# Column halves of the array for nearly all matmuls of a window-attention and Fourier kernel

## The chip, the cores and the metric

The kernel runs on one core of a Trainium2 chip. The metric is device time in microseconds (us), from the first to the last instruction of one execution; lower is better. The core has a matrix engine (TensorE, "PE" in the profile, with its weight loads as "PEld"), a vector engine (VectorE, "DVE"), a scalar engine (ScalarE, "ACT"), GpSimd ("POOL"), and SyncE ("SP"), which issues the DMA transfers. TensorE computes `lhsT.T @ rhs`: a weight load puts `lhsT` into the array of 128 rows by 128 columns, then the columns of `rhs` stream through it, and the result goes to PSUM, which here is used as 8 banks of 512 f32 values per partition. [...]

## The reference

Input `x` has shape (32, 56, 56, 128) in f32: 32 images of 56 by 56 tokens with 128 channels. Two layers, each with a residual, everything in f32:

```python
# layer 0: group norm, shifted 7x7 window attention with 4 heads of 32 channels
qkv = (win @ w_qkv.T)...                       # win: windows of 49 tokens of roll(gn(x), (-3, -3))
attn = softmax(q * scale @ k.T + bias + mask)  # per window and head, 49 x 49
out = (attn @ v) @ w_proj.T + b_proj           # rolled back
x = x + out
# layer 1: group norm, a Fourier mix along width and along height, a feed-forward
xy = idct_w(einsum(dct_w(gn(x))[first 32 modes], w0))
xx = idct_h(einsum(dct_h(gn(x))[first 32 modes], w1))
x = x + relu((xx + xy) @ W1 + b1) @ W2 + b2    # 128 -> 512 -> 128
```

## The kernel before

An image is 8 rows of 8 windows. The kernel walks over 32 x 8 rows ("cycles"); in one cycle the parts of several stages, for different rows and images, stand side by side so that TensorE always has work. Each engine runs its instructions in the written order. The matmuls of one cycle come in groups by the part of the array that they use, and the functions have names after that: full (128 rows x 128 columns), half columns (128x64), quarters (64x64), eighths (64x32).

```python
CONV_BEGIN = NWR + 2        # NWR = 8: the cycle in which layer 1 of image 0 begins
def attn_bank(): return bank("pa", 4)      # PSUM: 4 banks for attention,
def conv_bank(): return bank("pc", 4)      # 4 for layer 1, each in turn

def attn_qk(im, i, first):                 # row i of image im
    pq = attn_bank()
    nc.tensor.matmul(pq[:, :n], lhsT=im.w[:, 0:C], rhs=src, ...)            # L363, n = 392 or 393
    nc.scalar.activation(q[:, :RT], pq[:, :RT], AF.Identity, ...)
    pk = attn_bank()
    nc.tensor.matmul(pk[:, :n], lhsT=im.w[:, C:2*C], rhs=src, ...)          # L370
    ...                                     # k copied by ScalarE, then by VectorE
def attn_v(im, i, r):                       # L395: 8 windows, on column halves
def attn_scores(im, i, r):                  # L417: 64x64; then VectorE adds bias and mask (L425)
def attn_max(r):                            # VectorE maximum (L435), GpSimd subtracts it (L436)
def attn_exp(r):                            # ScalarE (L442)
def attn_divide(r):                         # VectorE sum (L447), reciprocal, GpSimd product (L450)
def attn_transpose(im, i, r):
    for hf in range(2):
        pt = attn_bank()
        for h in range(NH):
            nc.tensor.transpose(pt[...], a[...], ident[:PW, :PW])           # L461, full
        aT = work.tile([P, 4, P], F32, tag="aT", name="aT")
        ...                                 # copied out by VectorE, then ScalarE
def attn_values(im, i, r):                  # L486: attention x v, 64 matmuls of 64x32
def attn_project(im, i):                    # L528: output projection, 128*112
def transform(...)                          # L637: cosine transform, column halves
def mix(...)                                # L671: mode mix, column halves
def modes_back(...)                         # L710: inverse transform, 64x64
def ff_in(im, g):                           # group g: 512 (five times), 320, 256 tokens
    for f in range(NF):
        ph = conv_bank()
        nc.tensor.matmul(ph[:, :n], lhsT=wff1[:, f*P:(f+1)*P], rhs=xff[:, t0:t0+n], ...)  # L753
        ...                                 # relu on ScalarE (L761)
def ff_out(im, g):
    for c, m in enumerate(chunks):          # m = 128 tokens, in the group of 320 a last one of 64
        for f in range(NF):
            nc.tensor.matmul(pf[:m, ...], lhsT=im.hid[f][:, c*P:c*P+m], rhs=wff2[:, f],
                             start=(f == 0), stop=(f == NF - 1))            # L773
...
# one cycle, from cycle CONV_BEGIN on
full_first(cycle, norm)      # attn_qk(cycle), statistics, ff_in, attn_divide(cycle - 1)
if not row(cycle - 2)[0]: ...
elif any(c in FF_AT for _, c in fourier(cycle)):        # 7 of 8 cycles
    quarters(cycle)          # attn_scores(cycle), modes_back
    attn_max(cycle)
    half_columns(cycle)      # attn_v(cycle), transform or mix
    eighths(cycle)           # attn_values(cycle - 2)
else:
    half_columns(cycle); quarters(cycle); eighths(cycle); attn_max(cycle)
full_last(cycle, norm)       # attn_transpose(cycle - 1), ff_out, attn_project(cycle - 2),
                             # transposes of the next image (L262), attn_exp(cycle)
```

Of the kernel before, what the change touches and what calls it, by code (L numbers as in the profile page):

```python
# [41 lines left out]
FF_GROUPS = (HB, HB, HB, HB, HB, 320, 256)  # L42
FF_AT = (7, 8, 9, 10, 12, 13, 14)
PW = JP + WT
CONV_BEGIN = NWR + 2


@with_exitstack
def swin_fourier_kernel(
# [23 lines left out]
    const = ctx.enter_context(tc.tile_pool(name="const", bufs=1))  # L73
    big = ctx.enter_context(tc.tile_pool(name="big", bufs=1))
    work = ctx.enter_context(tc.tile_pool(name="work", bufs=2))
    small = ctx.enter_context(tc.tile_pool(name="small", bufs=4))
    psum = ctx.enter_context(tc.tile_pool(name="psum", bufs=2, space=bass.MemoryType.PSUM))
    dram = ctx.enter_context(tc.tile_pool(name="dram", bufs=2, space=bass.MemoryType.DRAM))

# [11 lines left out]
    def chunks_of(t, b, n0, n1):  # L91

        tok = t[b].rearrange("h w c -> (h w) c")
        wrap = (S - SS) // 2
        if n0 < wrap:
            e = min(n1, wrap)
            part = tok[SS * S + n0 * TC : SS * S + e * TC].rearrange("(n p) c -> p n c", p=TC)
            yield n0, e, slice(0, TC), part
        if n0 <= wrap < n1:
            yield wrap, wrap + 1, slice(0, S), t[b, S - 1].unsqueeze(1)  # L100
            yield wrap, wrap + 1, slice(S, TC), t[b, 0].unsqueeze(1)
        if n1 > wrap + 1:
            a = max(n0, wrap + 1)
            t0 = (2 * a + SS) % S * S
            part = tok[t0 : t0 + (n1 - a) * TC].rearrange("(n p) c -> p n c", p=TC)
            yield a, n1, slice(0, TC), part


    def load_image(b):
# [53 lines left out]
            )  # L163
    nc.sync.dma_start(rpb[JP : JP + WT], rpb[0:WT])

    mask_sb = const.tile([P, 2, 2, WT], F32, tag="mask", name="mask")
    nc.vector.memset(mask_sb, 0.0)
    for hh in range(2):
        rows = slice(hh * JP, hh * JP + WT)
# [132 lines left out]
    def image_norm(im):  # L302
# [46 lines left out]
        nc.scalar.mul(im.w, wqkv, rstd)  # L349
        yield  # L350
        pb = attn_bank()
        nc.tensor.matmul(pb[:, 0:1], lhsT=wqkv[:, 2 * C :], rhs=nb, start=True, stop=True)
        im.bias = small.tile([P, 5], F32, tag="bqkv", name="bqkv")
        nc.vector.tensor_copy(im.bias[:, 2:3], pb[:, 0:1])
        yield
# [2 lines left out]
    def attn_qk(im, i, first):  # L358

        n = RT if i else RT + 1  # L360
        q, src = q_sb, im.xw[i][:, :n]
        pq = attn_bank()
        nc.tensor.matmul(pq[:, :n], lhsT=im.w[:, 0:C], rhs=src, start=True, stop=True)  # L363
        if i == 0:
            nc.scalar.mul(im.bias[:, 0:1], pq[:, RT:n], QS)
        nc.scalar.activation(  # L366
            q[:, :RT], pq[:, :RT], AF.Identity, bias=im.bias[:, 0:1], scale=QS
        )
        pk = attn_bank()
        nc.tensor.matmul(pk[:, :n], lhsT=im.w[:, C : 2 * C], rhs=src, start=True, stop=True)  # L370
        if i == 0:
            for u in range(2):
                nc.scalar.mul(im.bias[:, 3 + u : 4 + u], pk[:, RT:n], heads[:, u : u + 1])
        pk3 = pk[:, :RT].rearrange("p (w j) -> p w j", j=WT)
        nc.scalar.activation(  # L375
            k_sb[:, 0], pk3, AF.Identity, bias=im.bias[:, 3:4], scale=heads[:, 0:1]
        )
        if first:
            nc.scalar.activation(
                k_sb[:, 1], pk3, AF.Identity, bias=im.bias[:, 4:5], scale=heads[:, 1:2]  # L380
            )
        else:
# [71 lines left out]
    def attn_transpose(im, i, r):  # L454

        a = a_sb[r % 3]
        im.aT[i] = []
# [3 lines that stand above are left out]
                nc.tensor.transpose(  # L461
                    pt[:PW, h * P : h * P + PW],
                    a[:PW, h, 2 * hf : 2 * hf + 2].rearrange("p w j -> p (w j)")[:, :PW],
                    ident[:PW, :PW],
                )
            aT = work.tile([P, 4, P], F32, tag="aT", name="aT")
            src = pt[:PW].rearrange("p (m x) -> p m x", x=P)[:, :, :PW]
            if hf:
                nc.scalar.copy(aT[:PW, :, :PW], src)
            else:  # L470
                nc.vector.tensor_copy(aT[:PW, :, :PW], src)
            im.aT[i].append(aT)
# [48 lines left out]
    def attn_project(im, i):  # L521
# [3 lines left out]
        base = i // 2 * WS  # L525
        pp = attn_bank()
        for n in range(n0, n1):
            nc.tensor.matmul(  # L528
                pp[:TC, (n - n0) * C : (n - n0 + 1) * C],
                lhsT=oT[:, (n - base) * TC : (n - base + 1) * TC],  # L530
                rhs=wproj,
                start=True,
                stop=True,
            )
        piece = im.x[:, n0:n1]
        nc.vector.tensor_tensor(
# [9 lines left out]
    def attn_sums(im, i):  # L546
# [7 lines left out]
            op=ALU.add,  # L554
        )
        yield
        sq = work.tile([TC, 4, C], F32, tag="sq", name="sq", bufs=1)[:, : n1 - n0]
        nc.scalar.activation(sq, piece, AF.Square)
        nc.vector.tensor_reduce(
            im.part[:, 1, :, i],  # L560
# [7 lines left out]
    def fourier_stats(im):  # L568
# [7 lines left out]
        yield  # L576
        pg = attn_bank()

        nc.tensor.matmul(
            pg[:, : C // 2],  # L580
            lhsT=gmean,
            rhs=tot.rearrange("p k g -> p (k g)"),
            start=True,
            stop=True,
        )
        own = small.tile([P, 2, C // 4], F32, tag="own", name="own", bufs=1)
        nc.vector.scalar_tensor_tensor(
            out=own,
# [141 lines left out]
    def ff_in(im, g):  # L730
# [19 lines left out]
        im.hid = []  # L750
        for f in range(NF):
            ph = conv_bank()
            nc.tensor.matmul(  # L753
                ph[:, :n],
                lhsT=wff1[:, f * P : (f + 1) * P],
                rhs=xff[:, t0 : t0 + n],
                start=True,
                stop=True,
            )
            hf = work.tile([P, HB], F32, tag="hid", name="hid", bufs=NF)  # L760
            nc.scalar.activation(hf[:, :n], ph[:, :n], AF.Relu, bias=b1sb[:, f : f + 1])  # L761
            im.hid.append(hf)

    def ff_out(im, g):
# [5 lines left out]
        pf = conv_bank()  # L770
        for c, m in enumerate(chunks):
            for f in range(NF):
                nc.tensor.matmul(  # L773
                    pf[:m, c * C : (c + 1) * C],
                    lhsT=im.hid[f][:, c * P : c * P + m],
                    rhs=wff2[:, f],
                    start=(f == 0),
                    stop=(f == NF - 1),
                )
# [33 lines left out]

    images = {}

    def row(r):
# [10 lines left out]
            return [(c >= 6, c % 2 * 2 + j) for j in range(2)]  # L829
        return []  # L830

    def full_first(cycle, norm):
        last, j = row(cycle - 3)
        if last:
            sums = attn_sums(last, j)
            next(sums)
# [22 lines left out]
        if row(cycle - 1)[0]:  # L859
            attn_divide(cycle - 1)  # L860

    def half_columns(cycle):
        im, i = row(cycle)
        if im:
            attn_v(im, i, cycle)
        for im, c in fourier(cycle):
            if c == 0:
                for g in range(4):
# [19 lines left out]
                modes_back(im, width, g)  # L888

    def eighths(cycle):  # L890
        im, i = row(cycle - 2)
        if im:
            attn_values(im, i, cycle - 2)

    def transpose_next(cycle):


        im, i = row(cycle - 1)
        if im:
            attn_transpose(im, i, cycle - 1)  # L900

    def last_out(cycle):
        for im, c in fourier(cycle):
            if c in FF_AT:
                ff_out(im, FF_AT.index(c))

    def full_last(cycle, norm):
        transpose_next(cycle)
        next(norm)
        im, j = row(cycle - 2)  # L910
        if im:
            last_out(cycle)
            attn_project(im, j)
        next_image(cycle)
        if row(cycle)[0]:
            attn_exp(cycle)
        next(norm)

    def next_image(cycle):
        b, i = divmod(cycle, NWR)  # L920
        if b + 1 < NB:
            if i == 2:
                images[b + 1] = image_begin(b + 1)
            for j in {3: (0,), 4: (2,), 5: (4,), 6: (6,)}.get(i, ()):
                image_groups(images[b + 1], j)

    def first_rows(cycle, norm):
# [2 lines left out]
            attn_qk(im, i, True)  # L932
        if cycle:
            attn_exp(cycle - 1)
        last, j = row(cycle - 3)
        if last:
            attn_project(last, j)
        im2, i2 = row(cycle - 2)
        if im2:
            attn_transpose(im2, i2, cycle - 2)  # L940
# [2 lines left out]
        if im:  # L943
            attn_scores(im, i, cycle)
            attn_max(cycle)
        if im2:
            attn_values(im2, i2, cycle - 2)
        next(norm)
        if last:
            for _ in attn_sums(last, j):  # L950
                pass
# [2 lines left out]
        if cycle < NWR // 2:  # L954
            image_bias(im, 2 * cycle)
        next(norm)
        next_image(cycle)
        if cycle == CONV_BEGIN - 1:
            attn_exp(cycle)
            attn_project(im2, i2)  # L960
            transpose_next(cycle)
        next(norm)

    def nothing():
# [4 lines left out]
    with tc.manual_schedule(engines={ET.PE, ET.Activation, ET.DVE, ET.Pool}):  # L969
# [6 lines left out]
        for cycle in range(NB * NWR + CONV_BEGIN + FF_AT[-1] - NWR + 1):  # L976
            if cycle < CONV_BEGIN:
                first_rows(cycle, norm)
            else:
                full_first(cycle, norm)  # L980
                if not row(cycle - 2)[0]:
                    half_columns(cycle)
                    last_out(cycle)
                    quarters(cycle)
                elif any(c in FF_AT for _, c in fourier(cycle)):
                    quarters(cycle)
                    if row(cycle)[0]:
                        attn_max(cycle)
                    half_columns(cycle)
                    eighths(cycle)  # L990
                else:
                    half_columns(cycle)
                    quarters(cycle)
                    eighths(cycle)
                    if row(cycle)[0]:
                        attn_max(cycle)
                full_last(cycle, norm)
            b, i = divmod(cycle, NWR)
            norm = nothing()
            if i == NWR - 2 and b + 1 < NB:  # L1000
# [64 lines left out]
```

## Time and profile before

| | |
|---|---|
| time, median of 3 | 3666.67 us (3664.5 to 3670.33) |
| span of the profiled execution | 3661.5 us |
| TensorE clock granted | 0.997 of full |
| TensorE matmul records | 61184 |
| bytes moved by DMA | 388.93 MB, 106 GB/s |
| costliest groups: feed-forward output (L773) | 760.4 us busy, 6400 records |
| hidden layer (L753) | 710.7 us busy, 1792 records |
| transposes of the attention (L461) | 267.3 us busy, 2048 records |

An engine's busy time is the union of its instructions' intervals. Matmuls overlap in the array and the ends of their intervals are modelled, so what a matmul costs is read from the distance between the starts of neighbouring matmuls rather than from its length. In the lists of groups the shape behind the tile names is the part of the array used (rows*columns), and then the operand that streams (partitions x columns). L773 is line 773 of the kernel.

### The profile page before, as it was taken

Reading aid. Unit: us, or ns where it says so; the run is one execution under the profiler, and the core shown is the slowest. Engines: PE = TensorE matmul, PEld = TensorE weight load, DVE = VectorE, ACT = ScalarE, POOL = GpSimd, SP = SyncE. Lnnn points to the kernel's source line nnn. Section 1 sums busy time; section 2 is a strip of 40 time slices with the busy share of each in tenths; the row PEclk is TensorE's granted clock in tenths of the full one; section 3 lists DMA queues with packets and bytes.
Section 4 is the critical chain, followed back from the end, with each engine's and each line's share of the span. In section 5 each row is a group of like instructions: output and inputs, shape, how many; then the busy total and the mean of one; then the engine's idle time right before and its main releaser. Section 6 shows DMA issues by size and latency. Waiting matters only on the chain.

```text
span 3661.5 us, 139922 instructions
## 1 busy us (share of the span) xinstructions
PE 3603.5 (98%) x61184; PEld 2940.9 (80%) x61184; DVE 2224.1 (61%) x4739; ACT 2123.3 (58%) x4043; POOL 1372.0 (37%) x1421
## 2 busy tenths in 40 slices
PE   7899999999999999999999999999999999999999
PEld 5787888888888888888787888888887888888887
DVE  7766666566666566665666665666666666556641
ACT  5555555555655555565556555556555555655553
POOL 5433334333334333333333333334333333333321
PEclk9999999999999999999999999999999999999999
DMA  4334433443434444334434343443344343433333
GB/s 116 97 102 114 106 107 94 112 113 102 117 96 110 108 108 112 104 97 113 108 101 113 95 118 104 106 115 94 111 107 110 105 112 92 118 106 104 97 109 96
DMA packets 687268, 388.93 MB, mean 106 GB/s; under 512 B 39968, under 2 KB 657601, under 8 KB 686401
## 3 DMA queue, kind: packets, MB, share of 16 engines
q1 hardware_dynamic: 686045, 379.65, 38.3%
q8 instruction: 482, 7.90, 0.9%
q14 instruction: 130, 1.06, 0.1%
q10 hardware_dynamic: 611, 0.32, 0.0%
HBM read 218.29 MB, written 161.48 MB: 104 GB/s over the span
## 4 chain that ended last, share of the span: by engine, by line
PE 94%; ACT 2%; DVE 2%; DMA 1%; issue 1%; POOL 0%; SPq 0%; ACTq 0%; POOLq 0%; DVEq 0%
PE pc L773 19%; PE pc L753 17%; PE pa L395 7%; PE pa L461 7%; PE pc L671 6%; PE pc L637 6%; PE pa L528 6%; PE pa L417 6%; PE pa L486 5%; PE pa L363 5%; PE pc L710 5%; PE pa L370 4%; PE pa L262 2%; ACT k L375 1%; DVE k L383 1%
## 5 line engine op out<-in xcount | busy, mean ns | idle before, releaser
L773 PE MATMUL pc<-wff,hid 128*128 128x128 f32 x6400 | 760.4, 276 | 0.9 <-ACT hid L761 0.8
L773 PEld LDWEIGHTS pc<-wff,hid 128*128 128x128 f32 x6400 | 732.3, 190 | 9.4 <-issue 2.4
L450 POOL TENSOR_TENSOR a<-a,rs 128x784 f32<-128x784 f32 x256 | 389.5, 1522 | 874.0 <-DVE rs L449 869.5
L753 PE MATMUL pc<-xf,wff 128*128 128x512 f32 (+2 forms) x1792 | 710.7, 539 | 0.9 <-DVE xf L721 0.7
L753 PEld LDWEIGHTS pc<-xf,wff 128*128 128x128 f32 x1792 | 339.2, 190 | 310.1 <-issue 228.6
L761 ACT ACTIVATE hid<-pc,b1sb 128x512 f32<-128x512 f32 (+2 forms) x896 | 535.2, 644 | 83.0 <-PE pc L753 73.7
L436 POOL TENSOR_TENSOR a<-a,mx 128x784 f32<-128x784 f32 x256 | 389.2, 1520 | 437.0 <-DVE mx L435 430.6
L785 DVE TENSOR_TENSOR res<-pc,res 128x512 f32<-128x512 f32 (+3 forms) x257 | 144.0, 571 | 660.9 <-issue 476.9
L293 POOL TENSOR_TENSOR xl<-xl,bproj 112x512 f32<-112x512 f32 (+1 forms) x256 | 285.6, 1137 | 508.6 <-PE pa L262 508.6
L425 DVE TENSOR_TENSOR a<-pa,bm 128x392 f32<-128x392 f32 x512 | 259.5, 549 | 178.8 <-PE pa L417 178.7
L517 DVE TENSOR_SCALAR oT<-pa,bqkv 128x98 f32<-128x98 f32 (+2 forms) x768 | 170.4, 276 | 218.4 <-PE pa L486 218.4
L402 ACT COPY v<-pa 128x512 f32<-128x512 f32 x256 | 153.3, 599 | 256.9 <-PE pa L395 256.9
L743 POOL TENSOR_TENSOR res<-res,b2sb 128x512 f32<-128x512 f32 (+2 forms) x256 | 263.8, 1035 | 94.3 <-DMA res<-scr 94.3
L280 ACT COPY xw<-pa 128x392 f32<-128x392 f32 x128 | 62.3, 486 | 396.1 <-PE pa L262 396.1
L383 DVE TENSOR_SCALAR k<-pa,heads,bqkv 128x392 f32<-128x392 f32 x246 | 168.4, 685 | 202.4 <-ACT k L375 200.1
L417 PEld LDWEIGHTS pa<-k,q 64*64 64x64 f32 x8192 | 183.4, 132 | 133.6 <-DVE rs L449 45.5
L395 PE MATMUL pa<-wn,xw 128*64 128x128 f32 x4096 | 282.7, 281 | 3.9 <-DVE a L425 3.9
L366 ACT ACTIVATE q<-pa,bqkv 128x392 f32<-128x392 f32 x256 | 150.5, 588 | 218.8 <-PE pa L363 217.3
L461 PE MATMUL pa<-ident,a 113*113 113x113 f32 x2048 | 267.3, 273 | 5.3 <-POOL a L450 4.4
L442 ACT ACTIVATE a<-a 128x784 f32<-128x784 f32 x256 | 225.0, 879 | 74.2 <-POOL a L436 74.1
L395 PEld LDWEIGHTS pa<-wn,xw 128*64 128x64 f32 x4096 | 220.4, 137 | 53.8 <-ACT xw L275 16.2
L435 DVE TENSOR_REDUCE mx<-a 128x16 f32<-128x784 f32 x256 | 247.0, 965 | 5.5
(91 smaller groups left out, 6050.6 us busy)
## 6 DMA issues: line engine op xcount, KB each, us to landing
zscr<-z SPq DMA_DIRECT2D x512, 112.0 KB
htok<-scr SPq DMA_DIRECT2D x256, 196.0 KB
zT<-zscr SPq DMA_DIRECT2D x192, 256.0 KB
res<-scr SPq DMA_DIRECT2D x160, 256.0 KB
out_dram<-res SPq DMA_DIRECT2D x160, 256.0 KB
scr<-xl SPq DMA_DIRECT2D x128, 224.0 KB
xl<-in_x_dram SPq DMA_DIRECT2D x32, 784.0 KB
xl<-in_x_dram SPq DMA_DIRECT2D x32, 672.0 KB
```

Of the source, the lines that this page charges most:

```text
L293: nc.gpsimd.tensor_tensor(piece, piece, bproj.unsqueeze(1).to_broadcast([TC, e - a, C]), ALU.add)
L395: nc.tensor.matmul(pv[hs, j * C : (j + 1) * C], lhsT=im.xw[i][:, w * WT : w * WT + JP], rhs=im.w[:, 2 * C : 3 * C], start=True, stop=True,)
L417: nc.tensor.matmul(ps[hp][HALVES[e], pr * 2 * WT : (pr + 1) * 2 * WT], lhsT=q[cs, w * WT : w * WT + JP], rhs=k_sb[cs, :, w], start=True, s ...
L425: nc.vector.tensor_tensor(a[:, 2 * hp : 2 * hp + 2, :, 0:WT].rearrange("p u w j -> p w u j"), ps[hp][:, :RT].rearrange("p (w u j) -> p w u ...
L435: nc.vector.tensor_reduce(mx, a3, axis=AX.X, op=ALU.max)
L436: nc.gpsimd.tensor_tensor(a3, a3, mx.unsqueeze(2).to_broadcast([P, 2 * NWR, WT]), ALU.subtract)
L450: nc.gpsimd.tensor_tensor(a3, a3, rs.unsqueeze(2).to_broadcast([P, 2 * NWR, WT]), ALU.mult)
L461: nc.tensor.transpose(pt[:PW, h * P : h * P + PW], a[:PW, h, 2 * hf : 2 * hf + 2].rearrange("p w j -> p (w j)")[:, :PW], ident[:PW, :PW],)
L743: nc.gpsimd.tensor_tensor(res[:m, c0:c1], res[:m, c0:c1], b2sb[:m].unsqueeze(1).to_broadcast([m, c1 - c0, C]), ALU.add,)
L753: nc.tensor.matmul(ph[:, :n], lhsT=wff1[:, f * P : (f + 1) * P], rhs=xff[:, t0 : t0 + n], start=True, stop=True,)
L761: nc.scalar.activation(hf[:, :n], ph[:, :n], AF.Relu, bias=b1sb[:, f : f + 1])
L773: nc.tensor.matmul(pf[:m, c * C : (c + 1) * C], lhsT=im.hid[f][:, c * P : c * P + m], rhs=wff2[:, f], start=(f == 0), stop=(f == NF - 1),)
```

## The change

The change puts every matmul of the full array, except the transposes, on two column halves: a helper issues it as two matmuls of up to 64 weight columns each, with the same streamed operand, into the two halves of the partitions. The cycle then needs the full array only for transposes, and these are gathered: in every second cycle the transposes of two rows are done together, and those of the next image are done in two cycles instead of four. For that the attention product and the output projection run three rows behind the scores instead of two, layer 1 begins one cycle later, and `aT` has four buffers. Its purpose is that the array changes its shape less often. To make room in SBUF, the small tiles have two buffers instead of four, and the mask shares a work tile. The core of the diff (left out: the same replacement at the small statistics matmuls, the mask's tile, and the first rows):

```diff
-CONV_BEGIN = NWR + 2
+CONV_BEGIN = NWR + 3
-    small = ctx.enter_context(tc.tile_pool(name="small", bufs=4))
+    small = ctx.enter_context(tc.tile_pool(name="small", bufs=2))
+    def halved(dst, lhsT, rhs, start=True, stop=True):
+        for p in range(0, dst.shape[0], P // 2):
+            ps = slice(p, min(p + P // 2, dst.shape[0]))
+            nc.tensor.matmul(dst[ps], lhsT=lhsT[:, ps], rhs=rhs, start=start, stop=stop)
...
-        nc.tensor.matmul(pq[:, :n], lhsT=im.w[:, 0:C], rhs=src, start=True, stop=True)
+        halved(pq[:, :n], im.w[:, 0:C], src)
...
-        nc.tensor.matmul(pk[:, :n], lhsT=im.w[:, C : 2 * C], rhs=src, start=True, stop=True)
+        halved(pk[:, :n], im.w[:, C : 2 * C], src)
...
-            aT = work.tile([P, 4, P], F32, tag="aT", name="aT")
+            aT = work.tile([P, 4, P], F32, tag="aT", name="aT", bufs=4)
...
-            nc.tensor.matmul(
+            halved(
                 pp[:TC, (n - n0) * C : (n - n0 + 1) * C],
-                lhsT=oT[:, (n - base) * TC : (n - base + 1) * TC],
-                rhs=wproj,
...
-            nc.tensor.matmul(
-                ph[:, :n],
-                lhsT=wff1[:, f * P : (f + 1) * P],
-                rhs=xff[:, t0 : t0 + n],
+            halved(ph[:, :n], wff1[:, f * P : (f + 1) * P], xff[:, t0 : t0 + n])
...
-                nc.tensor.matmul(
+                halved(
                     pf[:m, c * C : (c + 1) * C],
-                    lhsT=im.hid[f][:, c * P : c * P + m],
-                    rhs=wff2[:, f],
+                    im.hid[f][:, c * P : c * P + m],
+                    wff2[:, f],
...
     def eighths(cycle):
-        im, i = row(cycle - 2)
+        im, i = row(cycle - 3)
...
+    def full(cycle):
+        for k in (2, 1) if cycle % 2 == 0 else ():
+            im, i = row(cycle - k)
+            if im:
+                attn_transpose(im, i, cycle - k)
+            if k == 2 and row(cycle)[0]:
+                attn_max(cycle)
+        next_groups(cycle)
+
+    def next_groups(cycle):
+        b, i = divmod(cycle, NWR)
+        if b + 1 < NB:
+            for j in {5: (0, 2), 6: (4, 6)}.get(i, ()):
+                image_groups(images[b + 1], j)
...
-    def full_last(cycle, norm):
-        transpose_next(cycle)
+    def halves_last(cycle, norm):
+        im, i = row(cycle)
+        if im:
+            attn_v(im, i, cycle)
+        if has_ff(cycle):
+            half_columns(cycle)
+        next_begin(cycle)
         next(norm)
-        im, j = row(cycle - 2)
+        im, j = row(cycle - 3)
         if im:
             last_out(cycle)
             attn_project(im, j)
-        next_image(cycle)
         if row(cycle)[0]:
             attn_exp(cycle)
...
-                full_first(cycle, norm)
-                if not row(cycle - 2)[0]:
+                halves_first(cycle, norm)
+                if not row(cycle - 3)[0]:
                     half_columns(cycle)
                     last_out(cycle)
                     quarters(cycle)
-                elif any(c in FF_AT for _, c in fourier(cycle)):
-                    quarters(cycle)
-                    if row(cycle)[0]:
-                        attn_max(cycle)
+                    continue
+                if not has_ff(cycle):
                     half_columns(cycle)
-                    eighths(cycle)
-                else:
-                    half_columns(cycle)
-                    quarters(cycle)
-                    eighths(cycle)
-                    if row(cycle)[0]:
-                        attn_max(cycle)
-                full_last(cycle, norm)
+                eighths(cycle)
+                quarters(cycle)
+                if row(cycle)[0] and cycle % 2:
+                    attn_max(cycle)
+                full(cycle)
+                halves_last(cycle, norm)
```

More of the change, by code (lines that the diff above doesn't have):

```diff
@@ L164, in swin_fourier_kernel @@
     nc.sync.dma_start(rpb[JP : JP + WT], rpb[0:WT])
-    mask_sb = const.tile([P, 2, 2, WT], F32, tag="mask", name="mask")
+    mask_sb = work.tile([P, 4, C], F32, tag="sq", name="mask", bufs=1).rearrange("p n c -> p (n c)")
+    mask_sb = mask_sb[:, : 4 * WT].rearrange("p (r k j) -> p r k j", r=2, k=2)
     nc.vector.memset(mask_sb, 0.0)
@@ L351, in image_norm @@
         pb = attn_bank()
-        nc.tensor.matmul(pb[:, 0:1], lhsT=wqkv[:, 2 * C :], rhs=nb, start=True, stop=True)
+        halved(pb[:, 0:1], wqkv[:, 2 * C :], nb)
         im.bias = small.tile([P, 5], F32, tag="bqkv", name="bqkv")
@@ L527, in attn_project @@
         for n in range(n0, n1):
-            nc.tensor.matmul(
+            halved(
                 pp[:TC, (n - n0) * C : (n - n0 + 1) * C],
-                lhsT=oT[:, (n - base) * TC : (n - base + 1) * TC],
-                rhs=wproj,
-                start=True,
-                stop=True,
+                oT[:, (n - base) * TC : (n - base + 1) * TC],
+                wproj,
             )
@@ L556, in attn_sums @@
         yield
-        sq = work.tile([TC, 4, C], F32, tag="sq", name="sq", bufs=1)[:, : n1 - n0]
+        sq = work.tile([P, 4, C], F32, tag="sq", name="sq", bufs=1)[:TC, : n1 - n0]
         nc.scalar.activation(sq, piece, AF.Square)
@@ L577, in fourier_stats @@
         pg = attn_bank()
-        nc.tensor.matmul(
[L580 to L585, printed above, removed]
+        halved(pg[:, : C // 2], gmean, tot.rearrange("p k g -> p (k g)"))
         own = small.tile([P, 2, C // 4], F32, tag="own", name="own", bufs=1)
@@ L752, in ff_in @@
             ph = conv_bank()
-            nc.tensor.matmul(
-                ph[:, :n],
-                lhsT=wff1[:, f * P : (f + 1) * P],
-                rhs=xff[:, t0 : t0 + n],
-                start=True,
-                stop=True,
-            )
+            halved(ph[:, :n], wff1[:, f * P : (f + 1) * P], xff[:, t0 : t0 + n])
             hf = work.tile([P, HB], F32, tag="hid", name="hid", bufs=NF)
@@ L772, in ff_out @@
             for f in range(NF):
-                nc.tensor.matmul(
+                halved(
                     pf[:m, c * C : (c + 1) * C],
-                    lhsT=im.hid[f][:, c * P : c * P + m],
-                    rhs=wff2[:, f],
+                    im.hid[f][:, c * P : c * P + m],
+                    wff2[:, f],
                     start=(f == 0),
@@ L830, in back_groups, with halves_first @@
         return []
-    def full_first(cycle, norm):
-        last, j = row(cycle - 3)
+    def halves_first(cycle, norm):
+        last, j = row(cycle - 4)
         if last:
@@ L860, in full_first, with has_ff @@
             attn_divide(cycle - 1)
+    def has_ff(cycle):
+        return any(c in FF_AT for _, c in fourier(cycle))
     def half_columns(cycle):
-        im, i = row(cycle)
-        if im:
-            attn_v(im, i, cycle)
         for im, c in fourier(cycle):
@@ L890, in eighths @@
     def eighths(cycle):
-        im, i = row(cycle - 2)
+        im, i = row(cycle - 3)
         if im:
[L893 to L900, printed above, removed]
+            attn_values(im, i, cycle - 3)
+    def full(cycle):
[11 more added lines that the diff above has]
+                image_groups(images[b + 1], j)
     def last_out(cycle):
@@ L917, in full_last, with next_begin @@
         next(norm)
-    def next_image(cycle):
+    def next_begin(cycle):
         b, i = divmod(cycle, NWR)
[L921 to L925, printed above, removed]
+        if b + 1 < NB and i == 3:
+            images[b + 1] = image_begin(b + 1)
     def first_rows(cycle, norm):
@@ L934, in first_rows @@
             attn_exp(cycle - 1)
-        last, j = row(cycle - 3)
-        if last:
-            attn_project(last, j)
+        im3, i3 = row(cycle - 3)
+        if im3:
+            attn_values(im3, i3, cycle - 3)
         im2, i2 = row(cycle - 2)
@@ L945, in first_rows @@
             attn_max(cycle)
-        if im2:
-            attn_values(im2, i2, cycle - 2)
+        if im3:
+            attn_project(im3, i3)
         next(norm)
+        last, j = row(cycle - 4)
         if last:
@@ L956, in first_rows @@
         next(norm)
-        next_image(cycle)
+        next_begin(cycle)
+        next_groups(cycle)
         if cycle == CONV_BEGIN - 1:
             attn_exp(cycle)
-            attn_project(im2, i2)
-            transpose_next(cycle)
+            last, j = row(cycle - 1)
+            attn_transpose(last, j, cycle - 1)
         next(norm)
```

## The prediction

> **What bounds the kernel.** I read the page's busy shares first, then the chain that ended last, then the weight loads by shape, then TensorE's timeline over one period.
>
> ```profile
> PE 3603.5 (98%) x61184; PEld 2940.9 (80%) x61184; DVE 2224.1 (61%) x4739; ACT 2123.3 (58%) x4043; POOL 1372.0 (37%) x1421
> PE 94%; ACT 2%; DVE 2%; DMA 1%; issue 1%; POOL 0%; SPq 0%; ACTq 0%; POOLq 0%; DVEq 0%
> L773 PEld LDWEIGHTS pc<-wff,hid 128*128 128x128 f32 x6144 | 705.3, 192 | 5.5 <-issue 2.4 <-ACT hid L761 2.0 <-ACT z L679 0.3
> L395 PEld LDWEIGHTS pa<-wn,xw 128*64 128x64 f32 x4096 | 220.4, 137 | 53.8 <-ACT xw L275 16.2 <-DVE a L425 5.0 <-DVE st L284 2.2
> ```
>
> TensorE is busy 98% and carries 94% of the chain; no other engine passes 61%. So the time is a sum of TensorE intervals, and a change pays only where it shortens one. Busy shares cannot show that, because the modelled ends overlap; I use distances between starts, in the timeline of one row:
>
> ```profile
> 683.46 1.04 PE L461 MATMUL pa<-ident,a 113*113 113x113 f32 x8
> 684.34 3.75 PE L773 MATMUL pc<-wff,hid 128*128 128x128 f32 x32
> 687.93 0.82 PE L528 MATMUL pa<-wproj,oT 128*112 128x128 f32 x6
> 688.58 0.89 PE L262 MATMUL pa<-ident_x,xl 112*128 112x112 f32 x7
> 689.31 0.83 PE L363 MATMUL pa<-xw,wn 128*128 128x392 f32 x2
> 689.97 0.82 PE L370 MATMUL pa<-xw,wn 128*128 128x392 f32 x2
> 690.72 1.09 PE L395 MATMUL pa<-wn,xw 128*64 128x128 f32 x16
> 691.65 3.66 PE L671 MATMUL pc<-w1sb,y 128*64 128x128 f32 x64
> 695.24 0.91 PE L417 MATMUL pa<-k,q 64*64 64x98 f32 x32
> 696.08 0.81 PE L486 MATMUL pa<-aT,v 49*32 49x49 f32 x64
> ```
>
> Each line is a group with its start, its modelled length, the part of the array used (rows*columns) and the count. From start to start: L773 takes 3.59 us for 32 passes, 112 ns each (an f32 matmul is two passes in the records, a transpose one). L671 on column halves takes 3.59 us for 64, less about 0.09 at its end: 109.3 ns per **pair**, since two halves start about 7 ns apart and run together. So a pair of halves costs what one pass of the full width costs, or 2 to 3 ns less.
>
> Within a stage the steps in the records are constant: 84 ns per four passes of L417, 109.3 per pair of L395, 99 per transpose, 429 per L753 pass of 512 columns, 329 per pass of 392. What a stage takes beyond count times step is the price of changing shape. L417 above: 0.84 us against 8 x 84 = 0.67, so 0.16. A 128x64 stage: 0.15. The attention product L486 (64x32): 0.74 in an undisturbed row against 0.54, so 0.20. The full-width stage: about 0.20, of which 0.09 sits on its first transpose (189 ns, not 99). Over the image period 618 to 730 us (112.1 us) there are 34 stages; the steps sum to 105.2 us and the excess to 6.9 us: 6.0 for the 34 changes, 0.9 for true waits. Of those, 0.42 is one late attention product at 652.96 us, where VectorE was held by the normalisation statistics.
>
> [...] L528 to L363 (both full), or L395 to L671, lose nothing, while every change of shape loses 0.15 to 0.20 us. [...] A pass of 128 moving columns streams in about 107 ns here (429/512 x 128)[...]; the records give 112, and 109 where only 112 columns are loaded (L528, 128 columns streamed). [...]
>
> **The change part by part.** The period is 8 rows (one image); there are 32 images.
>
> 1. *Shape changes.* Before, each row goes through full, 64x64, 128x64, 64x32 (order varies): 0.20 + 0.16 + 0.15 + 0.20 = 0.71 us, 5.7 per image. The feed-forward group of 320 tokens ends in a 64-column chunk inside the full stage: two more changes, 0.34. Together 6.0. After, projections and feed-forward are halves too, so a row goes halves, 64x32, 64x64, and to full only in even rows, with two rows' transposes, or where the next image is transposed (rows 5 and 6, and 6 is even). 8 x (0.15 + 0.20 + 0.16) = 4.1, plus five full stages of 0.20: 5.1. Saved: 0.95 us per image, 30 us. The edge 64x32 to 64x64 does not occur before; I give it the 0.20 of 64x32 to full.
> 2. *Halved feed-forward output.* 192 full-width passes of L773 per image at 112 become pairs at 109.3: 0.5 us per image, 16 us. The 64-column chunk has one half and stays at 109 per pass.
> 3. *Halved qkv, hidden layer, output projection.* L753 at 429 ns [...] and L370 at 329 have no slack; L363's 339 should fall to 329. L528 is at 109 already. About 0.1 us per image, 4 us. Twice as many instructions are issued, but four per 109 ns is the rate of L671 now, so no cost.
> 4. *Product three rows behind, transposes in pairs.* No work changes. The product comes before the scores, right after the feed-forward input: its operands are ready a row earlier, and the 0.42 us wait of the statistics row should go. That is 0.4 us per image, 13 us.
> 5. *New waits.* In even rows four PSUM banks are asked for at once. Row of feed-forward with 512 tokens: qkv 1.3 + hidden layer 3.4 + product 0.9 + scores 0.8 puts the first transposes at 6.5 us, those of the row just before at 7.4. Their softmax product on GpSimd ends at about 6.2 us after the row's start (4.7 to 6.2 in the records), and VectorE has emptied the scores' two banks at 7.0 and 7.5 (0.55 us each). They fit with 0.1 to 1 us. In row 6 there is no feed-forward and the second image transpose needs a bank that VectorE empties only after its 0.97 us maximum: about 0.4 us late, 13 us in all. I let 4 and 5 cancel.
> 6. *One more row in flight.* One more thin row while filling: rows with attention alone take 7 to 9 us in the trace for about 5.7 of TensorE work (five stages' steps and changes as above), so +3.
>
> Sum: 30 + 16 + 4 - 3 = 47 us, and about 5 for waits that ease elsewhere: 3667 - 52 = **3615 us**, 1.4% less.
>
> **Rivals.**
> - *Waits take it back.* Four banks of attention PSUM, TensorE at 98%: a 0.5 us wait in each even row (bank or GpSimd's product) is 4 x 32 x 0.5 = 64 us, the whole gain, giving about 3680. For it: the slacks of 0.1 to 1 us above. Against it: VectorE is free 39%, and exp moves earlier, as it no longer queues behind the image copies on ScalarE.
> - *Wide halves do not run as pairs.* Every halved stage now streams at most 128 columns. If two tiles of 392 or 512 columns disturbed each other by 5%, L753 and the qkv (32 x 31 us) would lose 50 us: about 3665. Fully serial halves would add hundreds of us. For it: no run here shows a wide pair. [...]
> - *Changes cost less when the array is never full.* If a change between halves, 64x32 and 64x64 costs 0.10 rather than 0.15 to 0.20, 24 changes give another 1.5 us per image: 3565. Against: 64x64 to 128x64 costs 0.16 today with no full stage at either side.
> - *ScalarE or VectorE become the bound.* Neither gains work; at 58% and 61% I discard it.
>
> **Range and chances.** The step lengths are firm; the changes are known to about 0.04 us each (29 x 0.04 x 32 = 37 us at worst, one way), the waits to about 0.5 us per image (16 us). Range 3588 to 3650 us. Faster by over 2% means under 3593, which needs cheaper changes or vanished waits on top: 0.14. Slower by over 2% needs a wait of over 1 us in most even rows or serial halves: 0.04. Within 2%: 0.82.
>
> **What would show it.** In the changed kernel's timeline: 32 pairs of the feed-forward output in 3.5 us rather than 3.59; 512-wide pairs 429 ns apart; scores going straight to the v projection in odd rows; the 64x32 stage at about 0.74 us; the period at about 110.6 us. I am wrong if wide pairs are over 435 ns apart, if transposes in even rows start late behind GpSimd or a bank, or if the 64x32 to 64x64 edge is far from 0.20.

## The result: 1.5% slower, 3725 us instead of 3666

Median 3725.1 us (3711.39 to 3730.89) against 3666.34 us for the kernel before (3664.5 to 3670.33): ratio 1.0153, 95% interval 1.0124 to 1.0183. Predicted were 3615 us, in a range of 3588 to 3650.

The page after the change, busy shares and the chain that ended last:

```profile
PE 3575.8 (96%) x72064; PEld 2850.6 (77%) x72064; DVE 2209.7 (59%) x4738; ACT 2139.4 (57%) x4044; POOL 1371.3 (37%) x1421
PE 83%; DMA 7%; issue 2%; DVE 2%; POOL 2%; ACT 2%; SPq 1%; POOLq 0%; ACTq 0%; DVEq 0%
```

TensorE's busy time fell by 28 us while the span grew by 60. Its share of the chain fell from 94 to 83%, and 7% of the chain are now DMA transfers, which had 1%. The array works less and waits more. An undisturbed stretch from the end of one row to the start of the third shows the new order (start, modelled length, group):

```profile
1355.27 0.81 PE L493 MATMUL pa<-aT,v 49*32 49x49 f32 x64
1356.01 0.90 PE L424 MATMUL pa<-k,q 64*64 64x98 f32 x32
1356.84 1.85 PE L468 MATMUL pa<-ident,a 113*113 113x113 f32 x16
1358.62 1.09 PE L402 MATMUL pa<-wn,xw 128*64 128x128 f32 x16
1359.55 1.80 PE L636 MATMUL pc<-dct_h,htok 112*64 112x64 f32 x56
1361.18 3.67 PE L112 MATMUL pc<-wff,hid 128*64 128x128 f32 x64
1364.67 1.04 PE L112 MATMUL pa<-wproj,oT 128*64 128x128 f32 x16
...
1366.86 3.60 PE L112 MATMUL pc<-xf,wff 128*64 128x512 f32 x16
1370.40 0.81 PE L493 MATMUL pa<-aT,v 49*32 49x49 f32 x64
1371.14 0.91 PE L424 MATMUL pa<-k,q 64*64 64x98 f32 x32
```

L112 is the helper that issues halves. The feed-forward output takes 3.49 us for its 64 records, which are 32 pairs (1361.18 to 1364.67, where the projection starts), 109 ns a pair; eight 512-wide pairs take 3.54 with the change of shape at their end. The 64x32 stage takes 0.74 us, and from the scores to the transposes it is 0.83. All of this is what the steps of the prediction said.

Over 27 periods in the middle of the run, counted from the starts in the trace, one image looks like this:

| us per image | before | after |
|---|---|---|
| steps (count times distance of starts) | 105.2 | 104.4 |
| changes of shape | 6.0 (34 stages) | 5.1 (29 stages) |
| waits (the rest of the period) | 1.0 | 4.5 |
| period | 112.2 | 114.0 |

The gain came, 1.7 us per image, and 3.5 us of new waits came with it. 27 x 1.78 = 48 of the 60 us lie in these periods, and the other 12 in the five periods' worth of rows at the two ends; at the rate of the middle, 5 x 1.78 = 9 of these 12 would be the same waits, which is an estimate.

Some of the 3.5 us is not waiting but slower work. Six times in these periods TensorE's granted clock stands at 0.50 for 3.41 us, each time just behind a pause with 2.05 to 2.72 us between two starts; eight more pauses of over 2 us have no such stretch behind them. The kernel before, whose longest pause there has 1.3 us between starts, has none. The first stretch (the 0.50 is the clock; then two groups of its timeline):

```profile
1162.46:1165.87 3.41, 3.41 (x20) 3.41 (x20) 2.38 (x5) 2.09 (x5) 2.12 (x4) 0.50 0.43 125
...
1163.66 2.60 PE L269 MATMUL pa<-ident_x,xl 112*128 112x112 f32 x14
1166.18 0.98 PE L402 MATMUL pa<-wn,xw 128*64 128x128 f32 x14
```

The 14 transposes of the next image take 2.52 us there, and 1.66 in the row at 1389.70. Against the same matmuls in the other images a stretch costs 1.4 to 1.7 us, and the six cost 9 of the 48 us.

TensorE's longest waits after the change (total us, times, longest):

```profile
PE pa L468 <- ACT oT L526: 38.1, 32, 2.5
PE pc L709 <- DMA zT<-zscr: 37.3, 34, 2.6
PE pc L636 <- issue: 24.9, 21, 2.3
```

The first two come about once per image, the third in two images of three. Before the change the largest of these totals was 9.3 us, and `zT` had 0.4:

```profile
PE pa L352 <- DVE nb L346: 9.3, 2, 4.7
...
PE pc L710 <- DMA zT<-zscr: 0.4, 1, 0.4
```

The three are the subject of the experiments.

**Wait 1, the attention's transposes on ScalarE.** The timeline of the row without feed-forward, with the other lines left out:

```profile
1384.19 4.68 SPq L680 DMA_DIRECT2D zscr<-z  x8
...
1384.48 0.59 ACT L678 COPY z<-pc 128x512 f32<-128x512 f32 x1 [0.29 <-PE pc L670]
...
1385.97 0.90 PE L424 MATMUL pa<-k,q 64*64 64x98 f32 x32
...
1386.96 0.59 ACT L678 COPY z<-pc 128x512 f32<-128x512 f32 x1 [1.90 <-PE pa L424]
...
1387.45 0.46 ACT L526 ACTIVATE oT<-pa,bqkv 128x196 f32<-128x196 f32 x1
...
1388.05 0.72 PE L468 MATMUL pa<-ident,a 113*113 113x113 f32 x5 [1.17 <-ACT oT L526]
```

The height mix writes four `z` tiles and there are three buffers. The fourth copy, at 1386.96, idles ScalarE for 1.90 us. The label names the scores, which `z` does not depend on; in the totals of ScalarE's waits the same copy stands as waiting for the DMA writes of `z`, 52.1 us after the change and 30.1 before:

```profile
ACT z L678 <- DMA zscr<-z: 52.1, 34, 3.2
...
ACT z L679 <- DMA zscr<-z: 30.1, 31, 2.7
```

Behind it on ScalarE, at 1387.45, is `oT`, which empties the bank that the transposes want. Before the change the scores and only then the attention product came between the mix and the transposes; now the product is first, and its emptying is stuck behind the fourth copy.

**Wait 2, modes on their way through DRAM.** The mixed modes go to DRAM (`zscr`) and come back transposed (`zT`). From the end of the last `z` copy of the width mix to the start of the first inverse transform the trace has 9.0 us before. Now the mix stands at the end of its row and the inverse transform early in the next, 7.4 us later, and its second half starts only at 9.5 us on average, when its modes have come. One image of the changed kernel:

```profile
1306.17 0.59 ACT L678 COPY z<-pc 128x512 f32<-128x512 f32 x1 [0.29 <-PE pc L670]
...
1314.05 0.94 PE L709 MATMUL pc<-idctw,zT 64*64 64x112 f32 x32
...
1316.59 1.00 PE L709 MATMUL pc<-idctw,zT 64*64 64x112 f32 x32 [1.59 <-DMA zT<-zscr]
```

**Wait 3, "issue".** TensorE pauses inside the forward width transform although nothing that the profile knows is missing.

### The profile page after: what moved, and what is told of

It reads as the page before. It is cut to its first block, busy times and chain, and to the rows that moved or that the text cites. A ratio compares the mean times of both kernels' runs of the same rounds, so it can differ in the third digit from the quotient of the medians.

```text
span 3721.3 us, 161472 instructions
## 1 busy us (share of the span) xinstructions
PE 3575.8 (96%) x72064; PEld 2850.6 (77%) x72064; DVE 2209.7 (59%) x4738; ACT 2139.4 (57%) x4044; POOL 1371.3 (37%) x1421
## 3 DMA queue, kind: packets, MB, share of 16 engines
q8 instruction: 567, 9.29, 1.0%
## 4 chain that ended last, share of the span: by engine, by line
PE 83%; DMA 7%; issue 2%; DVE 2%; POOL 2%; ACT 2%; SPq 1%; POOLq 0%; ACTq 0%; DVEq 0%
PE pc L112 34%; PE pa L112 13%; PE pa L402 6%; PE pa L468 6%; PE pc L636 5%; PE pa L424 4%; PE pc L709 4%; PE pc L670 4%; PE pa L493 4%; DMA zT<-zscr 4%; PE pa L269 2%; DMA zscr<-z 2%; POOL xl L300 2%; DMA out_dram<-res 1%; DVE a L432 1%
## 5 line engine op out<-in xcount | busy, mean ns | idle before, releaser
L112 PE MATMUL pc<-wff,hid 128*64 128x128 f32 x12544 | 745.2, 274 | 1.3 <-ACT hid L754 1.0
L112 PE MATMUL pc<-xf,wff 128*64 128x512 f32 (+2 forms) x3584 | 718.2, 539 | 0.6 <-DVE xf L720 0.6
L112 PEld LDWEIGHTS pc<-wff,hid 128*64 128x64 f32 x12544 | 707.8, 138 | 7.9 <-ACT hid L754 4.3
L112 PEld LDWEIGHTS pc<-xf,wff 128*64 128x64 f32 x3584 | 286.0, 137 | 361.5 <-issue 281.1
L112 PE MATMUL pa<-xw,wn 128*64 128x392 f32 (+1 forms) x2048 | 393.9, 499 | 0.6 <-DVE a L432 0.6
L468 PE MATMUL pa<-ident,a 113*113 113x113 f32 x2048 | 243.9, 272 | 39.6 <-ACT oT L526 38.1
L493 PEld LDWEIGHTS pa<-aT,v 49*32 49x32 f32 x16384 | 172.0, 105 | 139.0 <-issue 69.4
L468 PEld LDWEIGHTS pa<-ident,a 113*113 113x113 f32 x2048 | 218.6, 181 | 60.7 <-issue 43.9
L112 PE MATMUL pa<-wproj,oT 128*64 128x128 f32 (+1 forms) x3584 | 249.0, 274 | 0.4 <-DVE oT L524 0.4
L454 DVE TENSOR_REDUCE sm<-a 128x16 f32<-128x784 f32 x256 | 245.8, 960 | 5.8 <-ACT a L449 4.9
```

What stands on the lines that cost most here:

```text
L112: nc.tensor.matmul(dst[ps], lhsT=lhsT[:, ps], rhs=rhs, start=start, stop=stop)
L454: nc.vector.tensor_reduce(sm, a3, axis=AX.X, op=ALU.add)
L468: nc.tensor.transpose(pt[:PW, h * P : h * P + PW], a[:PW, h, 2 * hf : 2 * hf + 2].rearrange("p w j -> p (w j)")[:, :PW], ident[:PW, :PW],)
L493: nc.tensor.matmul(po4[u][h * HD : (h + 1) * HD, 2 * f + e], lhsT=v[ks, 2 * f + e, h * HD : (h + 1) * HD], rhs=im.aT[i][f][ks, h, e * JP : ...
```

## The experiments

Theory: the halves and the order do what was computed, and three waits, each from a buffer or a transfer that the new order brings too close, take more than the gain. Rival 1: halving itself is slow, with 18% more TensorE instructions (61184 matmul records to 72064). Rival 2: the paired transposes, with four PSUM banks at once. All ratios are against the kernel before, run on the same chip.

**One buffer more for the height mix.** The fourth `z` tile borrows the buffer of `sq`, another work tile.

```diff
-        z = work.tile([P, 4, C], F32, tag="z", name="z", bufs=3)
+        if not width and g == 3:
+            z = work.tile([P, 4, C], F32, tag="sq", name="z", bufs=1)
+        else:
+            z = work.tile([P, 4, C], F32, tag="z", name="z", bufs=3)
```

> The changed kernel, with a fourth buffer for the height mix: its last group's copy goes to another tile instead of waiting for the first group's DMA write. Theory (waits on buffers and transfers, made by the new order, eat the gain): the 1.2 us wait per image ahead of the paired transposes in the row without feed-forward goes, about 3725 - 38 = 3687 us. Rival 1 (halving and its longer TensorE instruction stream cost the time): within 8 us of 3725. Rival 2 (the four PSUM banks that two rows' transposes ask for at once): the wait stays, within 10 us of 3725.

Measured 3691.53 us, ratio 1.0061 (1.0046 to 1.0076). TensorE's waits now begin so:

```profile
PE pc L712 <- DMA zT<-zscr: 39.3, 34, 3.9
PE pc L636 <- issue: 27.5, 21, 2.0
```

The wait before the transposes is gone and the other two are untouched: 34 us for one buffer. Rival 2 falls for this wait, since the four banks are asked for as before.

**The width mix earlier.**

```diff
                 halves_first(cycle, norm)
+                mix_columns(cycle)            # mix(im, True, g), taken out of half_columns
```

> The changed kernel, with the two width mixes moved from the end of their rows to right behind the feed-forward input. Theory: the modes have 6 us more for their way through DRAM, the wait of the inverse width transform (1.5 us per image) goes, about 3725 - 47 = 3678 us. Rival 1: within 10 us of 3725. Rival 2: within 10 us of 3725, as no bank and no transpose is touched.

Measured 3680.9 us, ratio 1.003 (1.0009 to 1.0051).

```profile
PE pa L468 <- ACT oT L526: 39.2, 32, 2.2
PE pc L636 <- issue: 21.1, 18, 2.3
```

The wait for `zT` is gone; the modes now have 12.9 us. The wait for `oT` is as in the changed kernel, so the two are independent.

**The loads of columns later.** The first two of four loads, each two transfers of 196 KB, go behind the width transform, on ScalarE's queue; the other transfers' issue order moved a little with them.

```diff
-                load_columns(im, 0)
-                load_columns(im, 1)
...
                 for g in range(4):
                     transform(im, True, g)
+                load_columns(im, 0, nc.scalar)
+                load_columns(im, 1, nc.scalar)
```

> The changed kernel, with the first two loads of columns (4 transfers, 196 KB per pair) issued behind the forward width transform instead of at the start of that row. Theory: TensorE's pause inside that transform, 0.86 us per image, which no data dependency explains, comes from instruction fetches standing behind these loads in the DMA engines; it goes, about 3725 - 27 = 3698 us. If the fetch is late because of the number of instructions alone (rival 1), the pause stays within 0.2 us and the time within 8 us of 3725.

Measured 3719.43 us, ratio 1.0136 (1.0115 to 1.0157): a miss in size, 6 us instead of 27.

```profile
PE pc L709 <- DMA zT<-zscr: 40.2, 35, 3.4
PE pa L468 <- ACT oT L526: 36.5, 31, 2.5
...
PE pc L636 <- issue: 9.6, 9, 1.8
PE pc L636 <- DMA htok<-scr: 9.1, 11, 5.3
```

The pause left the width transform altogether, but the row after it paid: its height transform now pauses or waits for the columns themselves, 0.6 us per image.

**All three edits.**

> All three edits together. Theory: the waits are independent and add up, 3725 - 38 - 47 - 27 = about 3613 us, that is 1.5% under the kernel before. Rivals 1 and 2: 3700 us or more. If the waits hide behind one another, between 3640 and 3690 us.

Measured 3638.07 us, ratio 0.9917 (0.9902 to 0.9931), 25 us above the 3613 expected: the two large waits add up, and the third edit gives 6 us of its 27. This already beats the kernel before.

**Halves alone, and the order alone.** First the kernel before with the `halved` helper and nothing else:

> The kernel before in its own order, with only the matmuls halved as in the change. Theory (a pair costs no more than one full pass, a change of shape about 0.17 us): the image has 47 stages instead of 34, 13 x 0.17 = 2.2 us more, the shorter steps give 0.6 us back, so 32 x 1.6 = +51: about 3720 us, and up to 3735 if the longer instruction stream pauses more often. Rival 1 (halving itself costs what the change lost, on top of the shape changes): 3780 us or more.

Measured 3712.62 us, ratio 1.0117 (1.0099 to 1.0135). One row of its timeline shows why halves cost in the old order:

```profile
2004.21 1.09 PE L400 MATMUL pa<-wn,xw 128*64 128x128 f32 x16
2005.24 0.81 PE L491 MATMUL pa<-aT,v 49*32 49x49 f32 x64
2005.97 1.05 PE L466 MATMUL pa<-ident,a 113*113 113x113 f32 x8
2006.95 3.71 PE L112 MATMUL pc<-wff,hid 128*64 128x128 f32 x64
```

The transposes stand alone at full width, and take 0.98 us from start to start where eight steps of 99 ns are 0.79; the feed-forward output behind them takes 3.54 us where 32 pairs at 109 ns are 3.49. The trace has 48 stages per image (47 were expected) and a period of 113.8 us.

Then the changed kernel with the helper issuing one full matmul again:

> The changed kernel in its new order, with every halved matmul put back on the full array. Theory: 40 stages per image instead of 29, 11 x 0.17 = 1.9 us, and 0.6 us for the longer steps, 32 x 2.5 = +79 on 3725: about 3800 us, as the transfers' waits stay. If the longer rows hide part of the waits, 3760. Rival 1: 3725 us or less, as the halves are gone.

Measured 3771.15 us, ratio 1.0276 (1.0261 to 1.0291), with 40 stages as expected; the time lies between the 3800 expected and the 3760 for waits that longer rows partly hide.

```profile
PE pa L466 <- ACT oT L524: 25.8, 30, 2.3
PE pc L634 <- issue: 24.8, 19, 2.3
PE pc L707 <- DMA zT<-zscr: 14.1, 20, 2.6
```

All three waits are there without a single new half and with fewer TensorE instructions, the two for data smaller than in the changed kernel and the pause as large. So the order makes them, and rival 1 falls: within the new order the halves gain 46 us (3771 to 3725).

| median us | old order | new order |
|---|---|---|
| full matmuls | 3666 | 3771 |
| halves | 3713 | 3725 |

**The first two edits without the third, and with a split third.**

> The changed kernel with the fourth buffer of the height mix and the early width mix, the loads of columns left as in the change. Theory with additive waits: 3725 - 34 - 44 = about 3647 us (measured gains of the two single edits), and the pause in the forward width transform stays at 0.8 us per image. If the late column loads were what helped the run with all three edits, this one is at 3665 or more.

Measured 3644.23 us, ratio 0.9932 (0.9916 to 0.9947): additive, as expected.

> As the last, but of the first two loads of columns one is issued early and one behind the width transform, on ScalarE's queue. Theory (the instruction fetch stands behind the burst of transfers): with half of the burst on either side, both pauses shrink, 0.8 to about 0.3 us in the width transform and 0.45 to about 0.2 in the height transform: about 3630 us. If the fetch is late whatever the transfers are, 3647 us as the last.

Measured 3632.24 us, ratio 0.9897 (0.988 to 0.9913). "Issue" waits in the transforms fell from 27.5 us to 9.9, as expected.

**What the pause is.** The page lists a DMA queue of the kind "instruction". Here is its line after the change, and then before:

```profile
q8 instruction: 567, 9.29, 1.0%
...
q8 instruction: 482, 7.90, 0.9%
```

The columns are packets, MB and share; a packet has 16 KB. 9.29 MB are 64.5 bytes for each of TensorE's 2 x 72064 records of matmuls and weight loads; before, 7.90 MB were 64.6 bytes for each of 2 x 61184. From this I read that the queue brings TensorE's instructions. In the changed kernel's records all 28 "issue" waits of over 0.15 us end 2.2 to 3.1 us after such a packet starts, and the packet before it lies 6.5 to 12.7 us back, against a median of 6.3 us. So I take the pauses for late instruction fetches. The kernel before has such pauses too: its product at 652.96 us stops after 7 of 64 matmuls:

```profile
652.96 0.28 PE L486 MATMUL pa<-aT,v 49*32 49x49 f32 x7
...
653.44 0.74 PE L486 MATMUL pa<-aT,v 49*32 49x49 f32 x57 [0.20 <-issue]
```

Why they are late in that row was tested by adding useless bytes:

```diff
         im.cols[g] = t
+        if g < 2:
+            spare = dram.tile([2, S, CH, C], F32, tag="spare", name="spare", bufs=4)
+            for r in range(2):
+                nc.sync.dma_start(spare[r], src[r, :, CH * g : CH * (g + 1)])
```

> The kernel with the fourth buffer and the early mix (3644 us), plus useless copies in DRAM of the same bytes right behind the first two loads of columns, 784 KB per image that nothing waits for. Theory (instruction fetches stand behind bursts of transfers): [...] the pause in the forward width transform grows from 0.96 to 2 to 4 us per image, and the time to between 3680 and 3750 us. If the pause has another cause: within 10 us of 3644, as no instruction depends on these bytes.

Measured 3626.57 us, ratio 0.9896 (0.9881 to 0.991): the opposite of what was expected. The pause in the width transform shrank from 0.96 to 0.41 us per image. SyncE's timeline shows what was overlooked:

```profile
1420.57 0.82 SPq L658 DMA_DIRECT2D htok<-scr  x2
1421.44 1.66 SPq L663 DMA_DIRECT2D spare<-scr  x2
1423.15 1.08 SPq L658 DMA_DIRECT2D htok<-scr  x2
1424.27 1.60 SPq L663 DMA_DIRECT2D spare<-scr  x2
```

The copies came between the loads. Issuing two copies takes SyncE 1.7 us, so the second pair of loads is issued 2.6 us after the first instead of 0.9. To separate spacing from bytes, the same copies were put behind all loads:

> As the run with useless copies, but all four copies are issued behind the four loads of columns instead of between them, so that the loads stand in the queue as in the kernel with 3644 us and 784 KB more behind them. Theory (a fetch waits for the transfers that are queued when it is asked for, so it is the density of issues ahead of it that counts, not the bytes of the row): the pause in the width transform is back at 0.9 us per image or longer, up to 3, and the time between 3640 and 3730 us. If it was the copies' bytes or the DRAM layout that helped in the other run: as there, about 3627 us, pause 0.4.

Measured 3649.06 us, ratio 0.9954 (0.9938 to 0.9971), the pause back at 0.90 us per image. With 784 KB more in both, only the run that spread the loads is better than the 3644 us (ratio 0.9932) without copies. In these runs the pause, 0.41 us with the copies between the loads and 0.90 with them behind, follows how densely the loads are issued and not the bytes of the row. That an instruction fetch waits for transfers queued before it is the reading that fits all five placements of the loads; when a fetch is asked for is not in the records, so this remains an inference.

**The next image's load one row later**, on top of the split loads:

```diff
-        if b + 1 < NB and i == 3:
+        if b + 1 < NB and i == 4:
```

> The kernel with the split column loads (3632 us), with the next image's load (1.4 MB) begun one row later. Theory: its burst no longer follows the width transform, the pauses left in that row and the next (0.33 and 0.17 us per image) shrink by half, -8 us: about 3624 us. If the image then arrives too late for its transposes in row 5, TensorE waits for it, over 3660 us.

Measured 3627.79 us, ratio 0.99 (0.9883 to 0.9916); the pause in the width transform fell from 0.33 to 0.22 us, and the image came in time. This is the version to keep: 1.0% under the kernel before, with the change's idea and its waits mostly removed. Its period is 111.1 us. Its ratio is that of the split loads alone (0.9897), so for this last edit no gain in time is shown; the gain over the kernel before is. The mean granted clock of its profiled run is 0.998, against 0.993 in the changed kernel.

## Why the prediction was wrong

By its own steps:

1. *Shape changes*: right. 29 stages instead of 34; the edge from 64x32 to 64x64 that no trace had shown was given 0.20 us and took 0.202, scores to halves 0.16, halves 0.15, the full stage 0.19. The runs put the price at 0.15 to 0.20 us a stage in every combination tried, and the run with halves alone paid it 14 more times per image. No run put the transposes on halves.
2. *Halved feed-forward output* and 3. *the wide matmuls*: right. Pairs at 109 ns, 512-wide pairs at 429, 392-wide at 329. Rival "wide halves do not run as pairs" is dead. Together with 1 they gave 1.7 us per image, where 1.55 had been computed.
4. *The 0.42 us of the statistics row should go*: wrong, and this was a misreading of the trace before. A stop after 7 of 64 matmuls of one group cannot be an operand or a bank, since the first matmuls had them. It goes with a late packet of the instruction queue, which starts 2.6 us before the product goes on and 12.9 us after the packet ahead of it. One image's 0.42 us was also taken for all 32; over the run these stops of the product came to 7.7 us, not 13. In the new order the pause, now in the width transform, grew to 0.9 us per image instead of going away.
5. *New waits*: this step failed, with the sentence "I let 4 and 5 cancel". Together they were priced at nothing, and measured were 3.5 us more of waits per image, 112 us over 32 images. It looked at PSUM banks and at GpSimd's product, and there it was nearly right: no wait for GpSimd, and 0.2 us per image where 0.4 was given for the bank at the image's transposes. It did not look at the SBUF buffers and the DRAM round trip of layer 1, as step 4 took it that "No work changes". Yet its place in the row did. The records allow 1.2 us per image for the fourth `z` copy and 1.5 for the returning modes; with 0.9 for the pause, 0.3 for the halved clock behind long pauses and 0.2 for the bank that is about 4.1 of the 4.5 us of waits. The first two could have been read off the profile before: ScalarE's wait for the writes of `z`, 30.1 us in 31 times, and the 9.0 us from mix to inverse transform. That a long pause can also slow the work behind it stood in no step.
6. *One more row in flight, +3 us*: of the right size. In the run with split loads, fill and end together took 628 us outside the 27 periods, and 631 before; at that run's gain of 1.0 us a period it would have been 626.

The rival "waits take it back" had the direction and, with 3680, not the size, and named the wrong waits. Slower by over 2% had 0.04 and did not happen either; the error was in giving the waits 0.5 us of uncertainty per image when only those of one kind had been checked.

With the two waits removed the kernel runs in 3644 us, and with a shorter pause in 3627 to 3632, in the upper part of the predicted range. What still separates it from 3615 is about 0.2 us per image for the bank, 0.2 us of pause, and smaller waits. The two buffers of the small tiles and the shared mask tile were in every run of the new order; what they cost was not measured apart, and lies within this rest.

## What to carry to other kernels

When the work of an engine at 98% is put in a new order, the time that hid every other loop moves too, so go through every buffer ring and every trip through DRAM whose two ends change places, even if their code is untouched, and compare the time they have in the old trace with the time left in the new order. Halves and order paid only together and with their waits removed: each alone was slower, and so were both with the waits. Where TensorE stops in the middle of a group that has begun to read its tiles and write its banks, and no releaser is named, look at the instruction queue: here all 28 "issue" waits of over 0.15 us in the changed kernel ended 2.2 to 3.1 us after a late packet of it started.

## What the runs showed of the hardware

- Two column halves of a 128x128 f32 matmul run as a pair, 7 ns between their starts, at the price of one full pass at these widths: 109 ns for 128 columns (full 112, or 109 with 112 weight columns), 216 for 256, 269 for 320, 329 for 392 (full 329 and 339), 429 for 512.
- A single 64-column chunk on one half, whose own passes are 109 ns apart, overlaps with the other half's next group: at 1308.36 us in the changed kernel projection matmuls of 48 columns start among the chunk's own, 6 to 44 ns behind them.
- The DMA queue of the kind "instruction" brought 64.5 bytes for each of TensorE's records, in 16 KB packets (567 packets, 9.29 MB), and in the changed kernel TensorE goes on 2.2 to 3.1 us after a late packet starts. Spreading the data loads that come before, even with useless copies, went with 13 to 18 us less here (ratio 0.9932 to 0.9896, 3644 to 3627).
- Behind some pauses of TensorE the granted clock falls to 0.50 for 3.41 us: in the changed kernel behind 6 of the 14 pauses of over 2 us in the middle of the run, at about 1.5 us each.
